# Products that share TensorE's array, given priority once the first of them is placed

## The chip, the cores and the metric

The kernel runs on one core of a Trainium2 chip. The metric is the device time of one execution in microseconds; the figure for a kernel is the median of its runs. The kernel before takes 9128.17 us (three runs, 9097.35 to 9143.35).

## The reference

The program computes four residual layers on a batch of 16 images of 192 channels and 32 x 32 pixels, all in 32-bit floats.

- Layer 0 is an mLSTM block over the 1024 pixels as a sequence (12 heads of 32), followed by a linear map, a 3 x 3 convolution, batch statistics and a leaky ReLU.
- Layer 1 is an attention with 6 heads whose queries and keys come from a small simulated circuit. For each pixel and head, six normalized numbers become the angles of a product state of 64 entries; two fixed 64 x 64 circuits (one for queries, one for keys) turn it into amplitudes, whose squares, summed with signs and projected, give 4 numbers per query and key. They are normalized, and the attention weight is the softmax over all 1024 pixels of minus the squared distance of query and key, divided by a temperature. The values are the 32 channels of the head.
- Layer 2 predicts, with a 3 x 3 convolution, 18 offsets per pixel, samples the image at the 9 displaced places with bilinear weights, multiplies by one weight per channel and tap, and adds up.
- Layer 3 maps 192 channels to 510 per half, scales 2 x 2 patches in the Fourier domain, runs a depthwise 3 x 3 convolution, multiplies the GELU of one half by the other and maps back to 192 channels.

Each layer begins with a normalization over groups of channels and ends in `x = x + ...`.

## The kernel before, in words

`network` runs three parts one after the other: `circuits` (the two circuits as matrices, once), `phase_a` (layer 0, all images) and `phase_b` (layers 1 to 3, all images). The change lies in `phase_b` alone.

**How phase B is written down.** Five generators produce its instructions: `vectors` (queries and keys of layer 1), `attention`, `offsets` and `gathers` (layer 2), and `layer3`. Each gives back a cost at every `yield`, and `weave` always continues the one whose costs, divided by the length it is given, have come least far. So the work of up to four images is recorded interleaved: one image's attention beside another's gathers and a third's layer 3.

**How the order on each engine comes about.** The tile framework gives each instruction a priority by its place in that record. A scheduler then fills each engine's queue: of the instructions that are ready in its own model of the machine, the one with the lowest priority number goes next. A pair of products recorded one after the other need therefore not stand together in the end: when the first is placed, something recorded earlier may become ready and be put between them. On the chip each engine runs its queue strictly in that order and waits at semaphores.

**Buffers in PSUM.** `big` hands out tiles of 128 x 1024 (two of them), `mm` tiles of 128 x 512 (two); `pav` and `pdef` have one of their own.

**The products that the change touches.** TensorE's array has 128 rows (the contraction) and 128 columns (the output's partitions). A product that needs less occupies part of it.

- `pcirc` (L1050, in `vectors`): two heads' states, each 64 rows, times a circuit matrix, into the two halves of one `big` tile; ScalarE squares it into `prob` (L1052).
- `pz` (L1061): signs and projection. Eight products per pair of heads, each 128 rows by 32 columns, for w (query or key), hf (half of the pixels) and hh (head); the four combinations of w and hf stand in the four column strips, and hh = 1 adds to hh = 0. The recorded order is hh, then w = 0, 1, then hf = 0, 1. VectorE or ScalarE adds the result to `zr` (L1067, L1069).
- `pmax` (L1146, in `attention`): queries by keys for 128 queries and 512 keys, two heads with 64 rows each; VectorE takes the largest (`mx`, L1148).
- `pscore` (L1185): keys by queries, two heads with 64 rows each; ScalarE takes the exponential (`pexp`, L1188).
- `pav` (L1177, in `weigh`): values times `pexp`, 128 rows by 64 columns per head, added up over eight blocks of keys. The columns beside the values hold ones, so that the sums come with it.
- `poffc` (L1311, in `layer2_offsets`): the offsets' convolution, 9 taps, each as four products of 96 rows by 32 columns in the four column strips.

Others on TensorE between them: `pmq` (L1154, a transpose of the maxima), `ppsi`, `paug`, `pv`, `pzt`, `pdt` (transposes), `pdef` (L1413, the sum over taps), `phad` (L1458) and `pout` (L1544) of layer 3. On VectorE: `acc` (L1407, L1409) weights the gathered rows `gt`, which GpSimd fetches by indirect DMA (L1366) and ScalarE begins to weight (L1374); `dc` (L1509) is the depthwise convolution.

Of the kernel before, what the change touches and what calls it, by code (L numbers as in the profile page):

```python
# [3 lines left out]

# [16 lines left out]
HS = 512  # L21
# [756 lines left out]
def phase_b(tc, d, out, ydram, stats, cn, nb):  # L778

    nc = tc.nc  # L780
    with ExitStack() as ctx:
# [154 lines left out]
        done = [nb] + [0] * 5  # L936
        g = SimpleNamespace(**locals())

        def stream(i, work):
            for b in range(nb):  # L940
                assert done[i] > b
                yield from work(g, b, left[b])
                done[i + 1] = b + 1
# [8 lines left out]
def vectors(g, b, left):  # L952
# [81 lines left out]
    for pr in range(3):  # L1034
        ps = []
        for hf in range(2):
            pt = mm("ppsi")
            for j in range(4):
                nc.tensor.transpose(pt[:, j * 128:(j + 1) * 128], psi[:, hf * 4 + j, :], cn.ident)
            ps.append(g.psit("psiT"))  # L1040
            nc.scalar.activation(ps[hf], pt, AF.Identity)
            yield 2.0
        prob = {}
        for w in range(2):
            for hf in range(2):

                pc = big("pcirc")
                for hh in range(2):
                    r = slice(hh * 64, hh * 64 + 64)
                    nc.tensor.matmul(pc[:, hh * HS:(hh + 1) * HS], cn.lqk[r, w, :], ps[hf][r, :], start=True, stop=True)  # L1050
                prob[w, hf] = v4("prob")
                nc.scalar.activation(prob[w, hf], pc, AF.Square)  # L1052
                yield 2.0

        pz = mm("pz")
        for hh in range(2):
            o = 20 - (pr * 2 + hh) * 4
            for w in range(2):
                for hf in range(2):
                    q = (w * 2 + hf) * 32  # L1060
                    nc.tensor.matmul(pz[q:q + 32, :], g.amat[:, w, o:o + 32], prob[w, hf][:, hh * HS:(hh + 1) * HS],  # L1061
                                     start=(hh == 0), stop=(hh == 1))
        yield 3.0
        if pr < 2:
            psi = products(pr + 1)
        if pr == 0:
            nc.scalar.activation(zr, pz, AF.Identity, bias=g.projb)  # L1067
        else:
            nc.vector.tensor_tensor(zr, zr, pz, ALU.add)  # L1069
        yield 1.0  # L1070
# [31 lines left out]
def attention(g):  # L1102
# [12 lines left out]
    def largest(i):  # L1115


        b, pr = pairs[i]
        assert g.done[1] > b
        qk, kr, vo = left[b].qk, left[b].kr, g.vo[pr]  # L1120
        qp, kp, kT, qT = g.qp, g.kp, g.kt_[i % 2], g.qt_[i % 2]
        xn = g.v4("xn")[:64]
        nc.sync.dma_start(xn, g.xnd[b, pr * 64:pr * 64 + 64, :])
        for hh in range(2):
            h, o = pr * 2 + hh, hh * 64
            nc.vector.tensor_copy(qp[:, :, o:o + 4], qk[:, :, 0, h, :])
            nc.vector.tensor_scalar_mul(kp[:, :, o:o + 4], qk[:, :, 1, h, :], g.rtau[:, 0:1])
            nc.vector.tensor_copy(kp[:, :, o + 4], kr[:, :, h])
        yield 2.0
        rows_of(kp, kT)  # L1130
        rows_of(qp, qT)
        yield 3.0
        pv = g.mm("pv").rearrange("p (t h e) -> p t h e", t=8, h=2)
        for tt in range(8):
            nc.tensor.transpose(pv[:, tt].rearrange("p h e -> p (h e)"), xn[:, tt * 128:(tt + 1) * 128],
                                cn.ident[:64, :64])
        for hh in range(2):
            nc.scalar.activation(vo[:, :, hh * 64:hh * 64 + 32], pv[:, :, hh, :], AF.Copy, scale=row("gate"))
        yield 2.0
        mx = p2.tile([128, 8, 2, 2], F32, tag="mx", name="mx")  # L1140
        for tt in range(8):
            for hf in range(2):
                pm = big("pmax").rearrange("p (h s) -> p h s", h=2)
                for hh in range(2):
                    r = slice(hh * 64, hh * 64 + 64)
                    nc.tensor.matmul(pm[:, hh, :], qT[r, tt * 128:(tt + 1) * 128], kT[r, hf * HS:(hf + 1) * HS],  # L1146
                                     start=True, stop=True)
                nc.vector.tensor_reduce(mx[:, tt, hf, :], pm, AX.X, ALU.max, negate=True)  # L1148
                yield 1.2

        mq = p2.tile([128, 16], F32, tag="mq", name="mq")
        nc.vector.tensor_tensor(mq.rearrange("p (h t) -> p t h", h=2), mx[:, :, 0, :], mx[:, :, 1, :], ALU.min)
        pm = g.mm("pmq")
        nc.tensor.transpose(pm[:16, 0:128], mq, cn.ident)  # L1154
        mr = p2.tile([16, 128], F32, tag="mr", name="mr")
        nc.scalar.activation(mr, pm[:16, 0:128], AF.Identity)
        nc.sync.dma_start(g.mxd[i].rearrange("h (t n) -> (h t) n", t=8), mr)
        for hh in range(2):
            nc.sync.dma_start(qT[hh * 64 + 5:hh * 64 + 6, :], g.mxd[i, hh:hh + 1, :])
        yield 1.0  # L1160
# [3 lines left out]
    def values(i):  # L1164

        b, pr = pairs[i]
        kT, qT, vo = g.kt_[i % 2], g.qt_[i % 2], g.vo[pr]
        for hf in range(2):
            s = slice(hf * HS, (hf + 1) * HS)
            po = []  # L1170

            def weigh(tt, pe, po=po):
                if tt == 0:
                    po.append(g.ps("pav"))
                for hh in range(2):

                    nc.tensor.matmul(po[0][hh * 64:hh * 64 + 64], vo[:, tt, hh * 32:hh * 32 + 64],  # L1177
                                     pe[:, hh * HS:(hh + 1) * HS], start=(tt == 0), stop=(tt == 7))

            last = None  # L1180
            for tt in range(8):
                ps = big("pscore")
                for hh in range(2):
                    r = slice(hh * 64, hh * 64 + 64)
                    nc.tensor.matmul(ps[:, hh * HS:(hh + 1) * HS], kT[r, tt * 128:(tt + 1) * 128], qT[r, s],  # L1185
                                     start=True, stop=True)
                pe = e4("pexp")
                nc.scalar.activation(pe, ps, AF.Exp)  # L1188
                yield 1.2
                if tt == 0:  # L1190
                    todo.sums()
                else:
                    weigh(*last)
                    if tt == 1:
                        yield from todo.ends
                last = tt, pe
                yield 1.2


            pc = p2.tile([128, HS], F32, tag="pavc", name="pavc", bufs=1)  # L1200
            rd = p2.tile([128, HS], F32, tag="rd", name="rd", bufs=1)
            parts = [(slice(0, 32), slice(32, 64)), (slice(96, 128), slice(64, 96))]

            def sums(last=last, weigh=weigh, po=po, pc=pc, rd=rd):
                weigh(*last)
                nc.scalar.activation(pc, po[0], AF.Identity)
                for num, den in parts:
                    nc.scalar.activation(rd[num, :], pc[den], AF.Ln)
                    nc.scalar.activation(rd[num, :], rd[num, :], AF.Exp, scale=-1.0)

            def ends(hf=hf, s=s, pc=pc, rd=rd):
                if pr + hf == 0:
                    left[b].x = g.xtile("att")
                att = left[b].x
                for hh, (num, den) in enumerate(parts):
                    h = pr * 2 + hh
                    nc.vector.tensor_tensor(att[(h % 3) * 32:(h % 3) * 32 + 32, h // 3, s], pc[num], rd[num, :],
                                            ALU.mult)
                yield 1.0
                if pr + hf == 3:  # L1220
                    for k in range(2):
                        x1 = g.v4("x1")[:96]
                        nc.sync.dma_start(x1, g.x1d[b, k * 96:k * 96 + 96, :])
                        nc.vector.tensor_add(att[:, k, :], att[:, k, :], x1)
                        nc.sync.dma_start(g.x2d[b, k * 96:k * 96 + 96, :], att[:, k, :])
                        yield 1.5
                    g.done[2] = b + 1

            todo.sums, todo.ends = sums, ends()
# [37 lines left out]
def layer2_offsets(g, b, left):  # L1267
# [37 lines left out]
    po = mm("poffc")  # L1305
    for t in range(9):
        dy, dx = t // 3, t % 3
        for k in range(2):
            for hf in range(2):
                q = (k * 2 + hf) * 32  # L1310
                nc.tensor.matmul(po[q:q + 32, :], g.woff[:, k, t, :],  # L1311
                                 xpad[:, k, hf * 16 + dy:hf * 16 + dy + 16, dx:dx + 32], start=(t == 0), stop=(t == 8))
        yield 2.0
    yield 3.0
    ot = g.xp("ot")
# [377 lines left out]
```

## Time and profile before

| what | value |
|---|---|
| median of three runs | 9128.17 us |
| the profiled execution | 9142.37 us, of which the span of instructions is 9140.6 |
| TensorE matmul busy (PE) | 7621.4 us, 83% of the span |
| VectorE busy (DVE) | 6933.0 us, 76% |
| ScalarE busy (ACT) | 4243.4 us, 46% |
| GpSimd busy (POOL) | 2070.9 us, 23% |
| TensorE clock granted, mean | 0.908 |
| DMA | 814.45 MB, 89 GB/s |

PE counts the time in which at least one matmul runs, so two that run side by side count once. PEld is the loading of weights into the array, which runs beside the matmuls. The granted clock is a share of full speed. A line of groups names the source line, the engine, the operation, the tile written and the tiles read, the shape and the count, then the busy time and the mean duration of one in ns, then the engine's idle time ahead of them and what ended it. In a product's shape, `64*128` is rows by columns of the array. An f32 product that isn't a transpose leaves two matmul records.

### The profile page before, as it was taken

To read this page: it belongs to the slowest core of one execution; us is meant where nothing else is said; L and a number is where in the kernel's file an instruction comes from. 1 tells how busy PE (TensorE), PEld (TensorE's weight loads), DVE (VectorE), ACT (ScalarE), POOL (GpSimd) and SP (SyncE) were. 2 spreads that over 40 slices of the span, in tenths; PEclk is the share of its full clock that TensorE was granted. 3 is DMA by queue.
4 is the path that set the end of the run, shared out by engine and by line. 5 is a ranking of instruction groups with operands and counts; after the bars stand their busy time and mean duration, and the time that the engine had idled before them with its cause. 6 is when DMAs were issued, how large, how long until landed. Compare 5 with 4: busy or idle time off the path is not lost. (4 is left out here: it accounts for less than half of the span.)

```text
span 9140.6 us, 91470 instructions
## 1 busy us (share of the span) xinstructions
PE 7621.4 (83%) x30512; PEld 3316.6 (36%) x30512; DVE 6933.0 (76%) x14313; ACT 4243.4 (46%) x7407; POOL 2070.9 (23%) x1680
## 2 busy tenths in 40 slices
PE   5999999999999968888888888888888888878743
PEld 2555555555555533323223223223223223223221
DVE  7777777777777745568778778788788788788778
ACT  3444444444445424545445445445455455454422
POOL 0101001000100000223233233233232232332452
PEclk9899999999999979998999999999998999999865
DMA  1111111111111120343343343343343343334352
GB/s 53 41 43 45 46 43 50 44 43 42 47 45 47 39 59 23 106 135 120 111 130 114 112 136 112 107 139 113 111 135 111 114 134 112 117 123 124 113 157 69
DMA packets 301029, 814.45 MB, mean 89 GB/s; under 512 B 47579, under 2 KB 164381, under 8 KB 300555
## 3 DMA queue, kind: packets, MB, share of 16 engines
q0 software_dynamic: 92160, 453.06, 15.8%
q1 hardware_dynamic: 208395, 355.55, 12.6%
q8 instruction: 239, 3.92, 0.2%
q14 instruction: 235, 1.93, 0.1%
HBM read 667.13 MB, written 132.94 MB: 88 GB/s over the span
## 5 line engine op out<-in xcount | busy, mean ns | idle before, releaser
L1366 POOL DMA_INDIRECT gt<-xg,ix x1152 | 1748.4, 1518 | 3918.3 <-DVE acc L1407 1753.6
L1407 DVE SCALAR_TENSOR_TENSOR acc<-gt,w,acc 128x192 f32<-128x192 f32 x3456 | 1218.6, 413 | 310.1 <-ACT acc L1374 307.7
L1146 PE MATMUL pmax<-kt,qt 64*128 64x512 f32 x3072 | 949.7, 685 | 320.2 <-DVE mx L1148 180.2
L1185 PE MATMUL pscore<-qt,kt 64*128 64x512 f32 x3072 | 938.4, 656 | 264.3 <-ACT prob L1052 121.5
L1374 ACT ACTIVATE acc<-gt,w 128x192 f32<-128x192 f32 x1152 | 493.5, 451 | 1368.1 <-DMA gt<-xg,ix 1184.2
L1148 DVE TENSOR_REDUCE mx<-pmax 128x2 f32<-128x1024 f32 x768 | 935.8, 1219 | 232.3 <-PE pmax L1146 230.0
L1188 ACT ACTIVATE pexp<-pscore 128x1024 f32<-128x1024 f32 x768 | 781.6, 1018 | 569.5 <-PE pscore L1185 567.7
L1177 PE MATMUL pav<-pexp,vo 128*64 128x512 f32 x3072 | 971.9, 660 | 64.5 <-ACT pexp L1188 59.9
L509 POOL COPY qbd<-qT 32x384 f32<-32x384 f32 x512 | 305.8, 597 | 2840.4 <-PE se L543 2755.5
L1509 DVE SCALAR_TENSOR_TENSOR dc<-pad,wdw,dc 128x512 f32<-128x512 f32 x1152 | 808.9, 748 | 26.8 <-ACT dc L1507 25.7
L1413 PE MATMUL pdef<-acc,ident 128*128 128x384 f32 x1152 | 595.3, 605 | 170.9 <-DVE acc L1409 169.5
L539 ACT ACTIVATE dm<-dm,wtm 128x128 f32<-128x128 f32 x1536 | 491.0, 389 | 346.8 <-DVE dm L495 267.9
L1146 PEld LDWEIGHTS pmax<-kt,qt 64*128 64x128 f32 x3072 | 267.7, 199 | 851.7 <-DVE mx L1148 355.5
L1185 PEld LDWEIGHTS pscore<-qt,kt 64*128 64x128 f32 x3072 | 270.3, 193 | 757.8 <-issue 236.2
L551 PEld LDWEIGHTS pintra<-v,pt 128*128 128x128 f32 x3072 | 427.7, 213 | 163.3 <-issue 70.8
L551 PE MATMUL pintra<-v,pt 128*128 128x33 f32 x3072 | 436.9, 291 | 2.5 <-DVE pt L546 2.4
L1413 PEld LDWEIGHTS pdef<-acc,ident 128*128 128x128 f32 x1152 | 200.8, 215 | 565.2 <-issue 292.8
L1177 PEld LDWEIGHTS pav<-pexp,vo 128*64 128x64 f32 x3072 | 173.4, 142 | 630.8 <-issue 482.8
L546 DVE SCALAR_TENSOR_TENSOR pt<-se,dm 128x512 f32<-128x512 f32 x384 | 263.4, 686 | 140.9 <-PE se L543 137.9
L543 PE MATMUL se<-qbd,kT 64*128 64x256 f32 x1536 | 291.1, 448 | 54.3 <-DVE pt L546 54.3
L1409 DVE TENSOR_TENSOR acc<-acc,wdef 128x384 f32<-128x384 f32 x576 | 318.3, 553 | 2.6
L1544 PE MATMUL pout<-gelu,wout 128*96 128x512 f32 x512 | 247.6, 628 | 78.9 <-DVE gelu L1532 70.5
(424 smaller groups left out, 12598.0 us busy)
## 6 DMA issues: line engine op xcount, KB each, us to landing
dm<-gd SPq DMA_DIRECT2D x128, 768.0 KB
xg<-xt SPq DMA_DIRECT2D x224, 192.0 KB
gt<-xg,ix POOLq DMA_INDIRECT x1152, 4.5
xb<-x_in SPq DMA_DIRECT2D x32, 384.0 KB
y<-ydram SPq DMA_DIRECT2D x32, 384.0 KB
x1d<-xb SPq DMA_DIRECT2D x32, 384.0 KB
xnd<-y SPq DMA_DIRECT2D x32, 384.0 KB
xn<-xnd SPq DMA_DIRECT2D x48, 256.0 KB
```

Source lines behind the costliest of these rows:

```text
L539: nc.scalar.activation(dm[:, h, :], dm[:, h, :], AF.Exp, bias=wtm[:, c, 64 + h:65 + h])
L551: nc.tensor.matmul(pa[:, hh * 33:hh * 33 + 33], pt[:, h * 128:(h + 1) * 128], v33[:, hh, :], start=True, stop=True)
L1146: nc.tensor.matmul(pm[:, hh, :], qT[r, tt * 128:(tt + 1) * 128], kT[r, hf * HS:(hf + 1) * HS], start=True, stop=True)
L1148: nc.vector.tensor_reduce(mx[:, tt, hf, :], pm, AX.X, ALU.max, negate=True)
L1177: nc.tensor.matmul(po[0][hh * 64:hh * 64 + 64], vo[:, tt, hh * 32:hh * 32 + 64], pe[:, hh * HS:(hh + 1) * HS], start=(tt == 0), stop=(tt = ...
L1185: nc.tensor.matmul(ps[:, hh * HS:(hh + 1) * HS], kT[r, tt * 128:(tt + 1) * 128], qT[r, s], start=True, stop=True)
L1188: nc.scalar.activation(pe, ps, AF.Exp)
L1366: nc.gpsimd.indirect_dma_start(out=gt, out_offset=None, in_=xg, in_offset=bass.IndirectOffsetOnAxis(ap=ix[:, c:c + 1], axis=0))
L1374: nc.scalar.activation(acc[:, j, :], gt[:, 0:192], AF.Copy, scale=w4[:, 0, c:c + 1])
L1407: nc.vector.scalar_tensor_tensor(acc[:, j, :], gt[:, cr * 192:(cr + 1) * 192], w4[:, cr, c:c + 1], acc[:, j, :], ALU.mult, ALU.add)
L1413: nc.tensor.matmul(po[:, 0:384], cn.ident, acc.rearrange("p j c -> p (j c)"), start=(t == 0), stop=(t == 8))
L1509: nc.vector.scalar_tensor_tensor(out, src, w, add, ALU.mult, ALU.add)
```

## The change

`phase_b` defines `together(n)`, which is a block of higher priority (the instructions recorded in it count as if they stood 1000 places earlier) when n is not zero, and does nothing for zero. In five groups of products the first is recorded as before and the others in such a block. In `pz` the order of w and hf is also turned round, and n is zero for the first product alone (hh = 0, w = 1, hf = 1).

```diff
+        def together(n):
+
+            return tc.high_priority(1000) if n else nullcontext()
+
+        g.together = together
...
                 for hh in range(2):
                     r = slice(hh * 64, hh * 64 + 64)
-                    nc.tensor.matmul(pc[:, hh * HS:(hh + 1) * HS], cn.lqk[r, w, :], ps[hf][r, :], start=True, stop=True)
+                    with g.together(hh):
+                        nc.tensor.matmul(pc[:, hh * HS:(hh + 1) * HS], cn.lqk[r, w, :], ps[hf][r, :],
+                                         start=True, stop=True)
...
-            for w in range(2):
-                for hf in range(2):
+            for w in (1, 0):
+                for hf in (1, 0):
                     q = (w * 2 + hf) * 32
-                    nc.tensor.matmul(pz[q:q + 32, :], g.amat[:, w, o:o + 32], prob[w, hf][:, hh * HS:(hh + 1) * HS],
-                                     start=(hh == 0), stop=(hh == 1))
+                    with g.together(hh * 4 + 3 - w * 2 - hf):
+                        nc.tensor.matmul(pz[q:q + 32, :], g.amat[:, w, o:o + 32],
+                                         prob[w, hf][:, hh * HS:(hh + 1) * HS], start=(hh == 0), stop=(hh == 1))
...
                     r = slice(hh * 64, hh * 64 + 64)
-                    nc.tensor.matmul(pm[:, hh, :], qT[r, tt * 128:(tt + 1) * 128], kT[r, hf * HS:(hf + 1) * HS],
-                                     start=True, stop=True)
+                    with g.together(hh):
+                        nc.tensor.matmul(pm[:, hh, :], qT[r, tt * 128:(tt + 1) * 128], kT[r, hf * HS:(hf + 1) * HS],
+                                         start=True, stop=True)
...
-                    nc.tensor.matmul(po[0][hh * 64:hh * 64 + 64], vo[:, tt, hh * 32:hh * 32 + 64],
-                                     pe[:, hh * HS:(hh + 1) * HS], start=(tt == 0), stop=(tt == 7))
+                    with g.together(hh):
+                        nc.tensor.matmul(po[0][hh * 64:hh * 64 + 64], vo[:, tt, hh * 32:hh * 32 + 64],
+                                         pe[:, hh * HS:(hh + 1) * HS], start=(tt == 0), stop=(tt == 7))
...
                     r = slice(hh * 64, hh * 64 + 64)
-                    nc.tensor.matmul(ps[:, hh * HS:(hh + 1) * HS], kT[r, tt * 128:(tt + 1) * 128], qT[r, s],
-                                     start=True, stop=True)
+                    with g.together(hh):
+                        nc.tensor.matmul(ps[:, hh * HS:(hh + 1) * HS], kT[r, tt * 128:(tt + 1) * 128], qT[r, s],
+                                         start=True, stop=True)
...
                 q = (k * 2 + hf) * 32
-                nc.tensor.matmul(po[q:q + 32, :], g.woff[:, k, t, :],
-                                 xpad[:, k, hf * 16 + dy:hf * 16 + dy + 16, dx:dx + 32], start=(t == 0), stop=(t == 8))
+                with g.together(k * 2 + hf):
+                    nc.tensor.matmul(po[q:q + 32, :], g.woff[:, k, t, :],
+                                     xpad[:, k, hf * 16 + dy:hf * 16 + dy + 16, dx:dx + 32],
+                                     start=(t == 0), stop=(t == 8))
```

More of the change, by code (lines that the diff above doesn't have):

```diff
@@ L1 @@
 import math
-from contextlib import ExitStack
+from contextlib import ExitStack, nullcontext
 from types import SimpleNamespace
```

## The prediction

> **What bounds the kernel now.** I read the page first: the busy shares and the granted clock.
>
> ```profile
> span 9140.6 us, 91470 instructions
> PE 7621.4 (83%) x30512; PEld 3316.6 (36%) x30512; DVE 6933.0 (76%) x14313; ACT 4243.4 (46%) x7407; POOL 2070.9 (23%) x1680
> ...
> PEclk9899999999999979998999999999998999999865
> ```
>
> TensorE is the busiest engine, VectorE is close behind, and TensorE's clock is rarely whole. All edited products belong to the second half of the program, where attention runs from about 3350 to 8600 us. I then cut the steady part of that half into stretches of one image each (from one image's `pzt` to the next) and read the busy times by stretch. The columns are the stretch and its length, then busy time of PE, PEld, DVE, ACT and POOL, then the granted clock, the DMA share and GB/s.
>
> ```profile
> 5476.40:5826.00 349.60, 290.41 (x1099) 102.64 (x1097) 281.58 (x566) 172.59 (x268) 105.93 (x73) 0.91 0.39 119
> 5826.00:6166.70 340.70, 282.67 (x1100) 99.94 (x1098) 281.61 (x566) 172.12 (x268) 106.90 (x73) 0.93 0.40 122
> 6857.30:7208.00 350.70, 287.75 (x1100) 102.23 (x1098) 281.40 (x565) 172.07 (x268) 107.77 (x73) 0.91 0.39 118
> 7208.00:7549.40 341.40, 283.40 (x1100) 100.28 (x1098) 281.53 (x565) 172.18 (x268) 105.49 (x73) 0.93 0.40 122
> ```
>
> An image takes some 346 us; PE works about 286 of them and DVE 281, each waiting about 60. Neither is the bound alone: each waits for the other in turn. The images do the same work (DVE and ACT agree to 0.5 us), yet those with clock 0.93 are shorter by about 9 us and their PE time by about 6.
>
> Third, the timeline of PE, for what a product costs alone and beside its partner. An f32 product leaves two records, so x2 is one product and x4 is a pair.
>
> ```profile
> 5010.75 1.12 PE L1185 MATMUL pscore<-qt,kt 64*128 64x512 f32 x2
> 5011.80 0.28 PE L1154 MATMUL pmq<-ident,mq 128*16 128x128 f32 x1
> 5012.01 1.12 PE L1185 MATMUL pscore<-qt,kt 64*128 64x512 f32 x2
> 5013.06 0.91 PE L1413 MATMUL pdef<-acc,ident 128*128 128x384 f32 x2
> ...
> 5016.87 1.02 PE L1185 MATMUL pscore<-qt,kt 64*128 64x512 f32 x4
> 5017.82 1.08 PE L1177 MATMUL pav<-pexp,vo 128*64 128x512 f32 x4
> 5018.83 1.07 PE L1311 MATMUL poffc<-xpad,woff 96*32 96x512 f32 x8
> ```
>
> From one start to the next: a lone `pscore` takes 1.05 us twice (5010.75 to 5011.80, 5012.01 to 5013.06), because `pmq` stands between the two heads; the whole pair at 5016.87 takes 0.95. The pair of `pav` takes 1.01 and four `poffc` 1.0. Heads side by side cost one slot, heads apart cost two.
>
> Fourth, the chain of waits from 8004 to 8600 us (shares of that stretch), then the groups of the same stretch.
>
> ```profile
> by line: issue 14.9%; DMA gt<-xg,ix 14.1%; DVE acc L1407 10.5%; DVE mx L1148 8.4%; DVE dc L1509 7.1%; PE pav L1177 4.6%; PE pscore L1185 2.8%; PE pmax L1146 2.8%; DVE acc L1409 2.7%; PE pout L1544 2.4%; ACT pexp L1188 2.1%; DMA x<-x3d 1.8%;
> ```
>
> ```profile
> L1177 PE MATMUL pav<-pexp,vo 128*64 128x512 f32 x364 | 115.9, 671 | 14.8 <-ACT pexp L1188 14.8
> L1185 PE MATMUL pscore<-qt,kt 64*128 64x512 f32 x364 | 115.5, 670 | 26.9 <-ACT prob L1052 10.2 <-DVE mx L1148 7.9 <-ACT pexp L1188 6.5
> ```
>
> Of 596 us the chain spends 27 on `pav` (which ran 116 in that stretch), 17 on `pscore` (of 116) and 17 on `pmax` (of 101): only 61 of 333 us, 18%, of the edited products' time lies on the path.
>
> **The change, part by part.** The arithmetic and every instruction stay. I compared the orders in which the two programs issue.
>
> (1) Pairs put together. In phase B before, 144 `pav` stand alone (72 broken pairs), after, 2. Of `pscore`, `pmax` and `pcirc` (64 rows each, sharing slots among themselves) the order makes 1786 slots before and 1741 after; 26 lone `pscore` remain. `pav` goes from 840 slots to 769, `pz` from 108 to 96, `poffc` from 145 to 144. By the slots above: 71 x 1.00 (the lone `pav` at 5622.90 ends its slot at 5623.90) + 45 x 1.05 + 12 x 0.97 + 1 x 1.0 = 131 us less TensorE time, about 10 us in each steady image. This is an upper end only if TensorE is late everywhere.
>
> How much of it reaches the end? Low end: the chain's share. 71 x 1.00 x 0.24 + 45 x 1.05 x 0.15 + the 12 `pz` at the same 0.2 = 17 + 7 + 2, about 26 us (0.2 of it). High end: the image table. About 6 us less PE time goes with 9 us less length, so PE time can carry over whole: 131. Between them, the row that says how much of VectorE's waiting is TensorE's doing, from the waits of DVE in 4000 to 8600 us:
>
> ```profile
> DVE acc L1407 <- ACT acc L1374: 253.3, 118, 4.7
> DVE mx L1148 <- PE pmax L1146: 121.1, 97, 3.7
> DVE x L1390 <- PE pdt L1387: 76.8, 33, 6.1
> DVE xo L1537 <- PE pout L1544: 69.5, 25, 3.2
> ```
>
> Of some 855 us of waits, PE ends about 308 directly and some 158 through ACT (`gnrs`, `rd`, `low`): 0.55. The gather's ACT step ends 253, which no faster TensorE shortens. I take 0.4, between 0.2 and 0.55 and nearer to these rows than to the table, whose differing PE time comes just after idle stretches: 131 x 0.4 = **52 us gained**. The other 79 us turn into TensorE idle time.
>
> (2) What the new idle time does to the clock. The records of the clock know two values, 1.0 and 0.5, in stretches of 3.4 us or whole multiples. From 4000 to 8600 us it stood at 0.5 for 758 us. I cut the stage into those windows and set PE's busy share of each against the next window's clock. At full clock, under 0.4 busy was always followed by half clock, 0.4 to 0.5 in 63% of 30 windows, 0.5 to 0.8 in 5% of 198; at half clock the return came mostly above 0.9. So a window that loses 1 of its 3.4 us (0.3) falls through if it stood between about 0.5 and 0.75. Of the 581 windows less than 0.97 busy, 226 stand from 0.5 to 0.8. So about 79 x 0.3 = 24 more half-clock windows of 3.4 us, each losing 1.7 us of PE work: 41 us if all of it is carried, 16 at the same 0.4. From below, nothing, or a gain of the same order if the windows happen to fall better (the clock of the images above varies from 0.91 to 0.93 with no change at all). I take **16 us given back**.
>
> [...]
>
> (3) `pz` is turned round. Its first product now needs the last `prob`, and the eight go together; before, one `pz` was issued up to 46 places ahead and held its PSUM buffer meanwhile (5632.34 to 5668). The lone one is followed by 0.47 us of waiting for DVE, so its slot is mostly hidden, and it is counted in (1). A PE blocked on the last `prob` is not to be feared: the order has the group where its seven stood. The freed buffer is worth nothing to a few us; I take nothing.
>
> (4) Everything else the scheduler moved. 1384 of 17026 PE instructions change place, most by one to three; on DVE 977 of 14315 (no more than 8 places), on ACT 205 (3), on SP 24 (1), on POOL none. No wait or DMA is added. What a product passes is delayed by the 6 to 7 ns between starts of a pair. Worst on DVE: L1509 and the `tot` form go up to 7 places earlier, so two of 0.75 us stand ahead of an `acc` once an image: 16 x 1.5 = 24 us against, if nothing hides it; the same in favour where something else moves forward. I take nothing.
>
> **Sum.** 52 - 16 = 36 us. Against the profiled execution's 9142.37 (span 9140.6 and some 2 us around it) that is 9106; the median of the three runs lies 14 lower, at 9128.17, so I forecast **9092**, 0.4% less. About 0.5% (46 us) is what a measurement of this kernel can tell from no change.
>
> **Rivals.**
>
> (a) TensorE is the bound everywhere and the saved slots carry through: 9128 - 131 = 8997. For it: the image table, where less PE time went with more than its own size. Against: the chain, with under a fifth of these products on it, and the gathers' 253 us. It begins for me at a gain of 70 us. Chance 0.2.
>
> (b) Slower: the clock gate takes more than the slots give. Place: the windows of 3.4 us in the attention stage. Price: between images at 0.93 and 0.91 the half-clock time differs by 0.04 x 347 = 14 us and the length by about 7 to 9, so some 0.5 us per us of half clock. It eats the 52 us from 104 us more half clock (30 windows, where I expect 24), and makes the kernel slower by 0.5% from 196 us (57 windows): the clock of 4000 to 8600 us would fall from 0.92 to about 0.90. Time then 9128 + 46 = 9174 and more. For it: idle time grows by a tenth. Against: it needs over twice the windows. Chance 0.09 beyond the bound.
>
> (c) Nothing to see: the order holds the pairs together but the slots saved all end in waits for DVE and the gathers, and the clock takes what is left: 9128, within 20 us either way. For it: TensorE's own 786 us of waiting in that stage. That the change doesn't do what it says I leave at almost no chance, since the new order shows the pairs, and pairs side by side already run in one slot. Chance 0.16.
>
> **How the numbers follow.** The forecast (10 to 70 us gained) has 0.55, about a quarter of it beyond 46 us. Faster by over 0.5%: 0.15 + 0.2 = 0.35. Slower: 0.09. Within: the rest, 0.56. The range takes in most of (a) and the near side of (c), 9003 to 9150; the forecast's own is 9058 to 9118.
>
> **What would show it.** Right: PE busy falls by 100 to 130 us, no lone `pav`, an image of about 343 us, waits of PE in the attention stage up by some 60 to 80 us, clock there 0.91 to 0.92. Wrong: PE's waits unchanged and images of 336 us (rival a); a clock of 0.90 or less (b). The first half of the program, to 3350 us, must not change.

## The result, and the profile after

The changed kernel takes 9176.66 us (median of 6 runs, 9162.36 to 9216.32), the kernel before 9127.04 beside it on the same chip. The ratio is 1.0055, 95% interval 1.0036 to 1.0073: **slower by 0.55%**, about 50 us, where 36 us less was forecast.

The page of the changed kernel, the lines that were read first of before:

```profile
span 9172.6 us, 91383 instructions
PE 7524.9 (82%) x30512; PEld 3295.4 (36%) x30512; DVE 6929.3 (76%) x14313; ACT 4239.2 (46%) x7407; POOL 2114.6 (23%) x1680
...
PEclk9899999999999979998998998998998998899865
```

PE is busy 96.5 us less (7621.4 before), almost as forecast, DVE and ACT do the same work as before, and yet the span is 32 us longer. POOL, which the change does not name, is busy 44 us more. The mean clock fell from 0.908 to 0.904; from 4000 to 8600 us it stood at half for 829 us instead of 758.

The stage cut by image, as before (length, then PE, PEld, DVE, ACT, POOL, clock, DMA share, GB/s):

```profile
5478.80:5833.40 354.60, 282.95 (x1100) 100.64 (x1098) 281.27 (x565) 172.06 (x268) 112.28 (x73) 0.90 0.38 117
5833.40:6179.10 345.70, 276.26 (x1099) 98.72 (x1097) 281.03 (x565) 171.78 (x268) 106.64 (x73) 0.92 0.39 120
6179.10:6521.50 342.40, 283.64 (x1099) 102.16 (x1097) 281.01 (x565) 171.83 (x268) 102.74 (x73) 0.90 0.40 121
6521.50:6874.20 352.70, 280.51 (x1100) 101.37 (x1098) 281.24 (x565) 172.20 (x268) 109.62 (x73) 0.91 0.38 117
6874.20:7231.40 357.20, 285.20 (x1099) 101.78 (x1097) 281.30 (x565) 172.42 (x268) 110.76 (x73) 0.89 0.38 117
7231.40:7584.60 353.20, 278.60 (x1099) 99.37 (x1097) 281.23 (x565) 172.18 (x268) 111.28 (x73) 0.91 0.38 118
```

The steady images are some 4 us longer (351.0 on average of these six, 346.9 of nine before), where 3 less was forecast, at the same DVE time. The slots are saved (PE some 276 to 285 us an image) and idle time has taken more than their place.

VectorE's waits from 4000 to 8600 us in the changed kernel:

```profile
DVE acc L1421 <- ACT acc L1388: 206.0, 92, 4.6
DVE mx L1158 <- PE pmax L1156: 103.9, 86, 3.9
DVE x L1404 <- PE pdt L1401: 96.6, 30, 5.3
DVE pad L1484 <- ACT low L1479: 79.5, 37, 3.1
```

Against before, VectorE waits less for `pmax` (121.1) and for ScalarE's `acc` (253.3), as a quicker TensorE would have it. But it waits longer for `pdt` (76.8 before) and for `low` (42.7). These two rows led to the causes. In the chain of waits of 8004 to 8600 us the edited products still have little:

```profile
by line: DMA gt<-xg,ix 11.8%; DVE acc L1421 10.9%; DVE mx L1158 9.5%; issue 9.4%; DVE dc L1523 7.4%; PE pav L1188 3.4%; PE pmax L1156 2.7%; PE pscore L1197 2.6%; DVE acc L1423 2.6%; PE pout L1558 2.4%; DMA x<-x3d 1.9%; ACT pexp L1200 1.5%; 
```

To find the places I laid the two traces side by side, instruction by instruction, each counted from the end of the first `mx` of its image, and averaged ten steady images (the fifth to the fourteenth). VectorE falls behind in two steps, at its `pad` (a wait 2.8 us longer, of which 1.2 stay after the next `mx`) and at its `x` 19 us into the image (1.9 us more). There it is 3.1 us behind; afterwards the difference moves between 2.2 and 5.6 us and ends at 4.4.

### The profile page after: what moved, and what is told of

It reads as the page before. It is cut to its first block, busy times and chain, and to the rows that moved or that the text cites. A ratio compares the mean times of both kernels' runs of the same rounds, so it can differ in the third digit from the quotient of the medians.

```text
span 9172.6 us, 91383 instructions
## 1 busy us (share of the span) xinstructions
PE 7524.9 (82%) x30512; PEld 3295.4 (36%) x30512; DVE 6929.3 (76%) x14313; ACT 4239.2 (46%) x7407; POOL 2114.6 (23%) x1680
## 5 line engine op out<-in xcount | busy, mean ns | idle before, releaser
L1380 POOL DMA_INDIRECT gt<-xg,ix x1152 | 1792.3, 1556 | 3909.7 <-DVE acc L1421 1749.6
L1197 PE MATMUL pscore<-qt,kt 64*128 64x512 f32 x3072 | 901.3, 655 | 279.8 <-ACT prob L1060 109.1
L1188 PE MATMUL pav<-pexp,vo 128*64 128x512 f32 x3072 | 902.4, 668 | 68.0 <-ACT pexp L1200 64.1
L1057 PE MATMUL pcirc<-psiT,lqk 64*128 64x512 f32 x768 | 225.4, 668 | 117.1 <-DVE mx L1158 43.2
```

Of the source, the lines that this page charges most:

```text
L1380: nc.gpsimd.indirect_dma_start(out=gt, out_offset=None, in_=xg, in_offset=bass.IndirectOffsetOnAxis(ap=ix[:, c:c + 1], axis=0))
```

## The experiments

In all of them but the changed kernel's own variant, the order of every engine in phase B is held, by dependencies that add no semaphore, to the order of the kernel before, with the moves named. So each run shows what one move on one engine does. Ratios are to the kernel before, run on the same chip. From here I write 0.1% as 9 us.

### Which engine's order is it?

**Pairs alone**: only TensorE's broken pairs are put together.

> The kernel before, with the order of VectorE, ScalarE, GpSimd and SyncE held instruction for instruction as it was; on TensorE alone the broken pairs (pav, pscore, pmax, pcirc, pz) are put together at the place of their last product, 6829 slots become 6686. Theory M (the pairs gain, and the scheduler's other moves take it away): 9070 to 9105, TensorE's waits for VectorE's mx stay at about 154 us, gather issues at 1518 ns mean. Theory C (a tighter TensorE idles more and its clock falls): 9130 to 9175, half-clock time in 4000 to 8600 us up by 50 us or more from 758. Theory G (VectorE, reaching its two-input steps earlier because TensorE's products reach it earlier, stretches the gather's issue on GpSimd): 9150 to 9190, gather issues at 1550 ns or more. Theory N (saved slots are hidden): 9110 to 9145 with clock and gathers unchanged.

Measured 9179.33, ratio 1.0058 (1.0042 to 1.0074). The pairs alone make the whole loss, so theory M falls. The half-clock time rose to 884 us, as theory C asked, and the time fits theory G; the gathers' issues, at 1536 ns on average of the whole run against 1518, stay below what G named. (This order joins all broken pairs, 143 slots; the changed kernel joins 129. Each pair stands at the place of its first product; the expectation has this wrong, and a later one corrects it.)

**Moves alone**: TensorE as before, the other engines in the changed order.

> TensorE's order held as in the kernel before (6829 slots, broken pairs and all); VectorE, ScalarE, GpSimd and SyncE get the order of the changed kernel. Theory M: slower, 9150 to 9220, as the moved instructions cost 50 us or more by themselves. Theories C and G: TensorE's order is what counts, so within 20 us of 9128. Theory N: 9155 to 9185, since the whole difference would lie in the moves.

Measured 9186.92, ratio 1.0073 (1.0053 to 1.0093), where theories C and G had expected no change. It mixes two orders that the scheduler had not fitted to each other. Since the changed kernel, which has both, is no slower than the pairs alone, this is not the price of the moves in the change.

**Clock held up**, without and with the pairs. The added products are these:

```diff
         nc.tensor.matmul(po[:, 0:384], cn.ident, acc.rearrange("p j c -> p (j c)"), start=(t == 0), stop=(t == 8))
+        for _ in range(FILL[b * 36 + n]):
+            nc.tensor.matmul(po[:, 384:512], cn.ident, cn.ident, start=False, stop=False)
```

> The kernel before in its own order, with 2600 products more (ident by ident, 128 columns, into 128 columns of the pdef bank that nobody reads, some 0.215 us each, 559 us together), issued ahead of TensorE's instructions that waited 0.5 us or more in its trace, to fill 70% of each of these waits. The kernel's own work is all there. If the half clock costs what I priced (0.5 us of time per us of half clock): the half-clock time of 4000 to 8600 us falls from 758 to under 250 us, and the time by 100 to 250 us, less what fillers in wrong places delay; 8880 to 9030. If the half clock is nearly harmless, because it falls into stretches where TensorE waits anyway: 9110 to 9250, fillers being only in the way.

> The same fillers at the same instructions, in the order with TensorE's pairs put together. Theory C (the clock takes what the pairs give): with the clock held up, the pairs give what was forecast, and this kernel is 30 to 60 us faster than the one with fillers in the order of before. Theory G or N: it is no faster than that one, within 15 us, or is slower.

Measured 9149.32, ratio 1.0022 (1.0008 to 1.0036), and 9172.09, ratio 1.0049 (1.0036 to 1.0063). Half-clock time fell from 758 to 300 and 423 us, and neither kernel became faster. This speaks against the clock as a general cost, but both runs are clouded: in seven of the ten steady images of the first, the added products themselves shifted VectorE so that the gather described next was stretched.

### The first place: a `pav` that held `pgv` back

In before the second `pav` of a pair stood just ahead of `pgv`. Put together, it passes the ten products between, in 11 images:

```diff
 L1177 pav, head 0
+L1177 pav, head 1
 L1458 phad x8
 L1185 pscore x2
-L1177 pav, head 1
 L45 pgv
```

> The order of the kernel before on every engine, but for 11 products: in each of 11 images the second pav that stood just ahead of pgv goes 11 places forward, next to its partner (11 slots saved of the 129). Theory S (one collision starts it all: pgv, gnrs and gnnm come 0.6 us sooner, VectorE's oe steps fall on the gather's issue, which takes 2.8 instead of 0.95 us and lands 3.6 us later; then TensorE waits for the late mx, falls to half clock, and pdt is late by 2 us): both steps appear, +1.2 and +2.2 us an image at VectorE's pad and x, and the time is 9155 to 9175. Theory T (the two steps are separate): only the first appears, 9135 to 9148. Theory C (the mass of saved slots lets the clock fall): 11 slots do nothing, 9115 to 9135. (Correction to the first expectation of the pairs alone: there each pair stands at the place of its first product, pz at that of its second.)

> All pairs put together as in the kernel with the pairs alone (9179), except those 11, which stand apart as before; the other engines in the order of before. Theory S: neither step appears, and the remaining 118 saved slots give 10 to 50 us: 9075 to 9125. Theory T: the second step stays, 9150 to 9170. Theory C: 9165 to 9185, half-clock time from 4000 to 8600 us stays near 884 us.

Measured 9150.43, ratio 1.0012 (0.9999 to 1.0024), and 9165.17, ratio 1.0029 (1.0013 to 1.0046). In the run of this move alone the first step is there (VectorE 1.2 us later after the next `mx`, in each image) and the second is not; in the run of all the others it is the reverse. So theory S, that one collision starts it all, falls, and theory T holds: the steps are separate.

The timelines of VectorE and GpSimd in image 8 show the first. Columns: start, duration, engine, line, operation, the idle time before it and what ended it. The kernel before:

```profile
5872.78 1.66 DVE L1470 SCALAR_TENSOR_TENSOR pad<-phad,fft,low 128x256 f32<-128x256 f32 x4
5874.35 0.41 DVE L1407 SCALAR_TENSOR_TENSOR acc<-gt,w,acc 128x192 f32<-128x192 f32 x1
5875.56 0.16 DVE L57 SCALAR_TENSOR_TENSOR gnnm<-gngm,gnrs 96x2 f32<-96x2 f32 x1 [0.80 <-ACT gnrs L49]
5875.64 1.28 DVE L1481 TENSOR_TENSOR oe<-pad 128x512 f32<-128x512 f32 x2
```

```profile
5875.51 0.95 POOL L1366 DMA_INDIRECT gt<-xg,ix  x1 [7.90 <-ACT acc L1374]
```

And with the one `pav` moved:

```profile
5870.61 1.66 DVE L1470 SCALAR_TENSOR_TENSOR pad<-phad,fft,low 128x256 f32<-128x256 f32 x4 [1.50 <-ACT low L1465]
5872.19 0.41 DVE L1407 SCALAR_TENSOR_TENSOR acc<-gt,w,acc 128x192 f32<-128x192 f32 x1
5872.79 0.16 DVE L57 SCALAR_TENSOR_TENSOR gnnm<-gngm,gnrs 96x2 f32<-96x2 f32 x1 [0.19 <-ACT gnrs L49]
5872.87 1.28 DVE L1481 TENSOR_TENSOR oe<-pad 128x512 f32<-128x512 f32 x2
...
5881.62 1.27 DVE L1470 SCALAR_TENSOR_TENSOR pad<-phad,fft,low 128x256 f32<-128x256 f32 x3 [2.76 <-ACT low L1465]
```

```profile
5873.34 2.77 POOL L1366 DMA_INDIRECT gt<-xg,ix  x1 [9.27 <-ACT acc L1374]
5880.41 0.45 ACT L1374 ACTIVATE acc<-gt,w 128x192 f32<-128x192 f32 x1 [4.75 <-DMA gt<-xg,ix]
5880.77 0.82 ACT L1465 ACTIVATE low<-phad,fft 128x256 f32<-128x256 f32 x2
```

The gather can be issued when VectorE's `acc` has read the old contents of its buffer. The profile names the last event before it, ScalarE's `acc`; but in both kernels the issue starts 0.75 us after the end of VectorE's (5874.76 to 5875.51, 5872.60 to 5873.34), and it still does where that `acc` is moved, below. `gnnm` waits 0.80 us for TensorE's `pgv` by way of ScalarE in before. In that gap the gather's issue began, 0.13 us ahead of the `oe` steps, and took 0.95 us. With `pgv` sooner, the gap is 0.19 us, `oe` starts 0.47 us ahead of the issue, and the issue takes 2.77 us, to 5876.11. In the kernel with all pairs, whose trace has both landings, this gather lands some 3.5 us later than in before; ScalarE's `acc` waits for it with `low` queued behind it, and VectorE's `pad` waits 2.76 us for `low`. A gain of 0.6 us at one wait became a loss at another.

That VectorE's steps hold the issue up, the traces show in two ways. In seven of ten steady images of the kernel of before with added products the gather began later still, 0.74 us after the first `oe`, and yet ended at the same place, 3.24 us after it, as the one that began at 0.47:

```profile
5165.44 1.28 DVE L1486 TENSOR_TENSOR oe<-pad 128x512 f32<-128x512 f32 x2
5166.18 2.50 POOL L1368 DMA_INDIRECT gt<-xg,ix  x1 [7.65 <-DVE oe L1486]
```

And of the 1152 gathers of the kernel before, all 319 whose issue began while VectorE stood idle took 0.94 to 0.96 us; so did all but four, of up to 1.47, of the 200 begun during a step with one input (the maxima, statistics and copies) or during the `pad` that reads `phad` from PSUM (28 issues, 0.94 to 0.95 us). All 137 issues of over 2 us began during another of VectorE's two-input steps.

The rows above agree with this: 0.95 us became 2.77 beside steps of VectorE, and stayed 0.95 where the issue came first. Of the 137 issues of over 2 us, 81 began during a `tensor_tensor` step and 56 during a `scalar_tensor_tensor` step. By what means VectorE's steps hold an issue up, and which step of the run lets it go, no run shows.

**The test**: move the `acc` that frees the buffer ahead of the four `pad`, in 11 images.

```diff
 L1407 acc (cr 2, j 1)
+L1407 acc (cr 3, j 0)
 L1470 pad x4
-L1407 acc (cr 3, j 0)
 L57 gnnm
```

> A control for the next one. The order of before, except that on VectorE, in 11 images, the fifth of the six acc steps of a tap (the last reader of a gather buffer) goes ahead of the four pad steps behind which it stood, so that the next gather is issued about 1.7 us sooner, clear of the oe steps. This gather does not collide in the kernel before, so all theories expect about no change, 9110 to 9135.

> All pairs together, and the same 11 acc steps moved forward on VectorE, so that the gather's issue is over before the oe steps begin. Theory S: the issue takes 0.95 us again and lands in time, neither step appears, and the time falls from 9179 to 9075 to 9125, below the kernel before. Theory T: about 9160. Theory C: 9165 to 9185, since the pairs and the clock are untouched by it.

Measured 9141.63, ratio 1.0007 (0.9993 to 1.0021), in the order of before: no change, as expected. With all pairs 9152.75, ratio 1.0009 (0.9995 to 1.0023): some 44 us of the 53 are gone, more than theory T's 20. Image 8 of that trace (the moved `acc` is the last of the four):

```profile
5852.91 1.40 DVE L1407 SCALAR_TENSOR_TENSOR acc<-gt,w,acc 128x192 f32<-128x192 f32 x4
5855.06 0.94 POOL L1366 DMA_INDIRECT gt<-xg,ix  x1 [6.06 <-DVE acc L1407]
5864.54 1.65 DVE L1470 SCALAR_TENSOR_TENSOR pad<-phad,fft,low 128x256 f32<-128x256 f32 x4
```

The gather is issued 0.75 us after the moved `acc`, in 0.94 us, the step at `pad` is gone (no wait, and the next `mx` 0.7 us earlier than in before), and the step at `x` stands at 2.2 us. Issues of over 2 us number 137 in before, 148 with the pairs, 136 here.

### The second place: a hole of 1.1 us and the half clock

In before another `pav` stood three places behind its partner, after two `pscore`, some 9 us into the image.

```diff
 L1177 pav, head 0
+L1177 pav, head 1
 L1185 pscore x2
-L1177 pav, head 1
 L1146 pmax x2
```

> The order of before on every engine but for one product in each of 11 images: the second pav that stood behind the two pscore some 9 us into the image goes three places forward, next to its partner (11 slots saved). Theory H (this one pair opens the hole: TensorE comes to its next pmax 1 us sooner, waits that much longer for VectorE's mx, the window of the clock falls to about 0.7 busy, and the half clock then falls on pqub, pav and pdt, for which VectorE waits): half clock from 13 to 24 us of most images, VectorE's wait for pdt there from 0.8 to 3 us, and 20 to 28 us more than before, 9148 to 9165. Theory W (the whole mass of saved slots is needed): no change, 9120 to 9140.

Measured 9159.75, ratio 1.0028 (1.0016 to 1.0041): **one pair in each of 11 images costs 26 us**, and theory H is right. TensorE in image 8, before:

```profile
5889.23 1.07 PE L1177 MATMUL pav<-pexp,vo 128*64 128x512 f32 x2
5890.23 1.13 PE L1146 MATMUL pmax<-kt,qt 64*128 64x512 f32 x4
5891.19 1.02 PE L1185 MATMUL pscore<-qt,kt 64*128 64x512 f32 x4
5892.15 1.07 PE L978 MATMUL pqub<-preproj,y 96*128 96x18 f32 x8
5893.85 1.13 PE L1146 MATMUL pmax<-kt,qt 64*128 64x512 f32 x4 [0.63 <-DVE mx L1148]
5894.91 1.51 PE L978 MATMUL pqub<-preproj,y 96*128 96x18 f32 x12
5896.35 1.08 PE L1177 MATMUL pav<-pexp,vo 128*64 128x512 f32 x4
5897.36 0.64 PE L1387 MATMUL pdt<-ident,df 128*96 128x128 f32 x4
```

And with the one pair put together:

```profile
5891.40 1.13 PE L1185 MATMUL pscore<-qt,kt 64*128 64x512 f32 x4
5892.46 1.07 PE L978 MATMUL pqub<-preproj,y 96*128 96x18 f32 x8
5894.65 1.60 PE L1146 MATMUL pmax<-kt,qt 64*128 64x512 f32 x4 [1.12 <-DVE mx L1148]
5896.17 2.75 PE L978 MATMUL pqub<-preproj,y 96*128 96x18 f32 x12
5898.85 1.97 PE L1177 MATMUL pav<-pexp,vo 128*64 128x512 f32 x4
5900.75 1.09 PE L1387 MATMUL pdt<-ident,df 128*96 128x128 f32 x4
```

The second `pmax` waits for VectorE's `mx` in both, but the wait grows from 0.63 to 1.12 us, and everything behind it takes nearly twice as long: `pqub` 2.75 for 1.51, `pav` 1.97 for 1.08. The same kernel's clock in that stretch is the third number from the end here (0.57, and 1.00 in before from 5894 to 5898.5):

```profile
5894.30:5902.30 8.00, 7.65 (x26) 4.27 (x28) 4.43 (x7) 0.00 (x0) 0.00 (x0) 0.57 0.01 2
```

and VectorE's `x` pays, in the kernel before and in this one:

```profile
5898.04 0.68 DVE L1390 TENSOR_TENSOR x<-x,pdt 96x512 f32<-96x512 f32 x1 [0.53 <-PE pdt L1387]
```

```profile
5901.88 0.68 DVE L1390 TENSOR_TENSOR x<-x,pdt 96x512 f32<-96x512 f32 x1 [3.57 <-PE pdt L1387]
```

The lone slot of `pav` had kept TensorE's clock up there: 1.00 with it, 0.57 without, in the two stretches above.

**Two tests on it**, both in the kernel with all pairs and the `acc` moved. One fills the hole with five useless products, the other with real work: the `pav` pair that stood ahead of `pdt` goes ahead of that `pmax`.

```diff
 L978 pqub x4
+L1177 pav x2
 L1146 pmax x2
 L978 pqub x6
-L1177 pav x2
 L1387 pdt x4
```

> The kernel with all pairs and the 11 acc steps moved (9153, half clock in most images at 13 to 24 us), with 5 products more in each of 11 images (ident by ident, 128 columns, 0.215 us each at full clock, into columns that nobody reads), issued just ahead of that pmax, into its wait of 1.12 us. The kernel's own work is all there. If the clock is what makes pdt late there: the half clock of that stretch is gone, VectorE's wait for pdt falls from 3 us to under 1, and the time falls by 20 to 35 us to 9115 to 9133. If it is the order of the products: no change, 9145 to 9165.

> The same kernel (all pairs, 11 acc steps moved) with real work in the hole: in 11 images the pair of pav that stood ahead of pdt goes eight places forward, ahead of that pmax; nothing is added. If the hole and its half clock are what costs there: pdt comes 2 to 4 us sooner, VectorE does not wait for it, and the time is 9100 to 9130. The other 107 saved slots by the chain's share of 0.2 would put it at the lower end, by nothing at the upper. If the clock is no matter: 9140 to 9155.

Measured 9120.15, ratio 0.9983 (0.9970 to 0.9995), and 9119.59, ratio 0.9988 (0.9977 to 1.0000), from 1.0009. Adding 55 products made the kernel faster by some 24 us, so it is the clock and not the order of the products. TensorE of the second kernel in image 8:

```profile
5855.61 1.07 PE L978 MATMUL pqub<-preproj,y 96*128 96x18 f32 x8
5856.60 1.08 PE L1177 MATMUL pav<-pexp,vo 128*64 128x512 f32 x4
5857.61 1.13 PE L1146 MATMUL pmax<-kt,qt 64*128 64x512 f32 x4
5858.67 1.51 PE L978 MATMUL pqub<-preproj,y 96*128 96x18 f32 x12
5860.03 0.62 PE L1387 MATMUL pdt<-ident,df 128*96 128x128 f32 x4
```

No wait, full clock, and `x` follows `pdt` without one. From 4 to 20 us of an image the half clock stands for 2.6 us in before, 5.5 with the one pair, 6.1 in the changed kernel and 1.4 in both of these.

**Both repairs in the changed kernel**, in its own order on all engines:

> The changed kernel in its own order on all engines (9177), with both moves: 11 acc steps on VectorE ahead of the four pad steps, 11 pairs of pav ahead of the pmax that waits for mx. If these two places are where the change lost its time: 35 to 60 us less than the changed kernel, 9100 to 9140. If the loss is spread over the order: 9160 to 9180.

Measured 9142.26, ratio 1.0006 (0.9991 to 1.0022), from 1.0055: 22 moves (11 `acc`, 11 pairs of `pav`) take back about 45 us.

### What the other saved slots give, and what the half clock costs elsewhere

> The order of before on every engine; all broken pairs put together but the 22 at the two places (the pav ahead of pgv, and the pav behind the two pscore 9 us into the image), so about 121 slots saved. This is the change's gain with both its losses left out. If 0.4 of a saved slot reaches the end, as I forecast: 48 us less, 9080 to 9095. By the chain's share of 0.2: 9100 to 9112. If what VectorE saves in front of one wait is spent at its next wait, for ScalarE or a gather: 9122 to 9142. If there are more places like the two: above 9145.

Measured 9136.58, ratio 0.9998 (0.9988 to 1.0008). Some 121 saved slots (the 143 but for the 22 at the two places) give 2 us, at most 11. In the trace, that of the slowest of its 12 runs (9166.64 us), VectorE waits less at two `mx` of each image (0.52 to 0.01 us at 94 us into it, 3.65 to 2.82 at 231), 1.3 us together, and more at the waits that follow: `gelu` from ScalarE (2.85 to 3.53), `acc` (3.80 to 4.21), `psi` (0 to 0.39), `x` (0.61 to 1.08). The traces of the pairs alone and of the kernel with both repairs show the same two gains and also longer waits for `gelu` and `psi`.

> The kernel with all pairs, the 11 acc steps and the 11 pairs of pav moved (9120; half clock 741 us from 4000 to 8600 us), with 2501 products more (ident by ident, 0.215 us each, 538 us together, into columns that nobody reads), which fill 65% of those 206 waits of TensorE of 0.8 us and more at which a half-clock stretch stood or began. If half clock costs 0.5 us per us wherever it falls, as I priced it: at least 300 us less half clock and 100 to 200 us less time, 8920 to 9020. If it costs only at few places like the one found: the half clock falls as much, and the time is 9090 to 9150.

Measured 9211.33, ratio 1.0076 (1.0057 to 1.0094), a spoiled run: some of the added products depended on ScalarE's `df`, and TensorE stood 62 us waiting for it.

> As the run before it (9211), without its flaw: there some of the added products had to wait for ScalarE's df and held TensorE and pdt up by 4 us an image. Here 1518 products (326 us) fill half of 158 waits of 0.8 us and more at which a half-clock stretch stood or began, none of them dependent on df. If half clock costs 0.5 us per us wherever it falls: some 200 us less half clock than 741 and about 100 us less time than 9120, 9010 to 9040. If it costs only at few places: half clock falls as much, and the time is 9100 to 9150.

Measured 9122.12, ratio 0.9988 (0.9977 to 0.9998), the same as without the products (0.9988). Half-clock time fell from 741 to 488 us and bought nothing that the measurement shows. The added products were not in the way: behind 150 of their 158 groups TensorE still waited.

## Why the prediction was wrong, point by point

The step that failed is the carried share of (1), and with it "I take nothing" of (4). In the terms of the sum: the 52 us gained were about 2, the 16 us given back to the clock were some 26 at one place, and the nothing of (4) was about 11 alone. Together that is a loss of 35 us where 50 were measured; the rest is open, below.

- **(1) The slots** were right: 6829 became 6700, and PE is busy 97 us less where 100 to 130 were forecast. **The share of 0.4 was wrong**: 121 of the slots give 2 us (up to 11), a share of at most 0.1. I took it from the rows of VectorE's waits, but what a wait for TensorE loses, the next wait for ScalarE or a gather gains, in the rows above. The waits of VectorE that TensorE ends were not time that TensorE could give back here. Rival (c) named this.
- **(4) "I take nothing"** looked only at what is delayed ("what a product passes is delayed by the 6 to 7 ns"). What counted is what comes sooner: one `pav` less ahead of `pgv`, and `oe` runs into the gather's issue. Eleven such moves cost about 11 us alone (interval -1 to 22; the step in the trace, 1.2 us in 11 images, gives 13). The scheduler's other moves show no price: the pairs alone (1.0058) and the changed kernel (1.0055) agree.
- **(2) The clock**: the amount was near (82 us more half clock forecast, 71 measured), but its price was wrong both ways. At 0.5 us per us, spread, I took 16 us. That price came from four images out of nine, among the longest and the shortest: over the eight with whole work, images at 0.93 are 6 us shorter than those at 0.91, not 7 to 9, and that the clock made them shorter was assumed. Elsewhere 253 us less of it bought nothing; at one place, 11 pairs with about 3 us more of it each lost 26 us, since there `pqub`, `pav` and `pdt` run back to back ahead of a step for which VectorE waits. Rival (b) had half the kind of loss and asked for 196 us; it took no mass, but the place. Its time, 9174 and more, came out by luck, since another collision added to it.
- Its windows were also measured wrongly there. Counting all of PE's records, the stretch of `pqub` stood at 0.8 to 1.0 busy in before and did not look near the edge. `pqub` streams 18 columns a product. Left out of the count, the lowest window there stands at 0.49 to 0.61 in nine of ten images in before, and at 0.43 in the tenth, the only one that then fell to half clock. With the one pair, eight images fell, after windows of 0.35 to 0.43, and two did not, after 0.47 and 0.48. (In six of the eight TensorE had waited there, 1.12 us and once 0.84; in two it had not, and the narrow products alone made the window thin.) Over the whole stage the windows of 0.5 to 0.8 at full clock that were followed by half clock go from 5% of 198 to 1% of 211 by this count, and in the changed kernel from 18 of 255 to 2 of 247. That it is the columns is argued from this, not tested by itself.
- **(3) `pz`**: not tried alone; it is among the 121 slots that give nothing.
- Of the signs that were to show it right, fewer lone `pav`, a clock of 0.91 from 4000 to 8600 us and waits of PE up (786 to 904 us, by 118 where 60 to 80 were named) came all the same, and the first half of the program stayed as it was (the first `mx` of phase B 4 us earlier); the images of 343 us did not come.

**What stays open.** The parts measured alone (+11, +26, -2) add to 35 us, the pairs together cost 53 (38 to 68); the intervals allow that they simply add, and also some 18 us of interplay. And the changed kernel repaired (1.0006) stands 16 us above the same repairs in the order of before (0.9988), with intervals that overlap. The repaired kernel in the order of before is the fastest seen, by 0.1 to 0.2%, so at best a small gain.

## What to carry to other kernels

Here two engines wait for each other in turn, and 121 slots saved on one gave 2 us (at most 11): follow a saved slot through the next wait of the other, and measure the carried share by one move before believing it. Ask of each moved instruction what will run sooner, and what that collides with: two moves per image made most of the difference here, and a hole could be closed with work that was there already. A lone half-used slot kept the clock up here (1.00 with it, 0.57 without) ahead of a chain for which VectorE waited.

## What the runs showed of the hardware that was not expected

- A gather's issue on GpSimd took 0.95 us or 2.77 us, depending on 0.6 us of difference against VectorE's two-input steps. Begun while VectorE was idle it took 0.94 to 0.96 us, 319 times of 319.
- A wait of 1.12 us was followed by half clock in five of six images; in before TensorE waited 0.63 us there in four of ten, and none of these four fell. The wait stood among products of 18 columns; counted without them, the windows ahead of half clock there were 0.35 to 0.43 busy. That these products do not keep the clock up was not tested by itself.
- The half clock was almost free over most of the stage: 253 us less of it, no time (ratio 0.9988 with and without).
